# Routing all tokens in the first round, and gathering sorted tiles by a table of one-hot products

## The chip, the core and the metric

The kernel runs on one core of a Trainium2 chip. The metric is the device time of one execution in microseconds (us), as the median of several runs. TensorE is called PE here, VectorE DVE, ScalarE ACT, GpSimd POOL and SyncE SP, as in the profile. POOL issues the indirect DMAs and SP all the others.

## The reference, cut to what matters

The input `x` is 2 x 2048 tokens of 256 numbers. Two layers follow one another; each normalizes `x`, computes an attention branch `s` and a feed-forward branch `g`, and adds `s * silu(g)`. Only the first layer is touched:

```python
xn = _layernorm(x)
s = _L0_attn_ref(xn, ...)     # 16 heads, window of 128, plus 64 pooled latent keys, gated
g = _silu(_L0_ffn_ref(xn, ...))
x = x + s * g
```

`_L0_ffn_ref` is a mixture of experts with one expert for each token:

```python
expert_idx = argmax(softmax(x @ Wr.T))          # 8 experts
for e in range(8):
    inter += (expert_idx == e) * gelu(x @ W1[e] + b1[e])    # 256 -> 1024
y = inter @ Wo + bo + x                         # 1024 -> 256
out = (y - mean(y)) * rsqrt(var(y) + 1e-12) * gamma + beta
```

The second layer (a bucketed attention block, and a two-deep transformer of its own as the feed-forward branch) takes the rest of the time.

## The kernel before

**Tiling.** The 4096 tokens are 32 tiles of 128 (`NT`), taken in 8 groups of 4 (`NG`, `GT`). The first layer runs in eight rounds, one for each group `g`: the attention of the group's four tiles, and beside it whatever else is due. For the experts the tokens are sorted by expert, each expert's part padded to whole tiles of 128, so there are 39 sorted tiles at most (`FT = NT + E - 1`), and all 39 are always computed.

**Order of the work.** The instructions of PE, DVE, ACT and POOL stand in the order in which the program emits them; SP's DMAs are placed by the framework. `in_turn` (L90) takes lanes, each a list of steps with weights and a stretch from `a` to `b` of the round, gives each step a position in its lane's stretch by the weights, and emits all steps in order of position. So two numbers place each piece of work, and the engines run it in that order, each stalling where something is not there yet. A step emits all its instructions at once.

**The steps of the first layer.**
- `prep(g)` (L429): LayerNorm of a group on DVE with the reciprocal root on POOL, transposes on PE into `stream`, the eight router logits of each token, and the one-hot choice `oh`.
- `head(g)` (L649): projections of queries, keys and latent keys. `attention(g)` (L896): scores, softmax, weighted sums, gate, output; tile n's result is stored at L891 in the lane of tile n+1.
- `route()` (L473): from `oh` of all tokens, each token's place in the sorted order (`ati`) and each sorted tile's expert (`exi`). `ranks` uses two products on PE, the rest is DVE.
- `send(t)` (L546): one indirect DMA, from POOL, writes the 128 normalized rows of tile t to their places in `xsort` in DRAM. There are 32. `xsort` is filled with zeros at the start, so that the padding is defined.
- `open_experts` and `expert_load(i)` (L555, L563): `Wo` once; for a sorted tile the expert number is read into a register, then `w` (1 MB) and the tile's rows `xs` (from `xsort`) are loaded by SP. `expert(i)` (L571) does the two products with gelu between, and the normalization, and stores to `ysort`. Its `begin` asks for tile i+1. The results are fetched from `ysort` by `ati` in the next layer's `gate_head` (L341).

**The schedule of before.** Preps 0 and 1 and head 0 come before the first scores. Preps 2 to 4 lie in round 0, preps 5 to 7 and `route` in round 1, the sends from 0.7 of round 1 to 0.56 of round 2; the experts begin at 0.64 of round 2. `shares` says how much of a round holds experts:

```python
shares = [0, 0, 0.36, 1, 1, 1, 1, 0.7]
weight = sum(w for w, _ in flow) / sum(shares)
```

The pool `xp` holds the normalized rows of all groups (`xn`, 32 KB in each partition) until `open_experts` closes it; the weights of the experts then take its room.

Of the kernel before, what the change touches and what calls it, by code (L numbers as in the profile page):

```python
# [7 lines left out]
F32 = mybir.dt.float32  # L8
# [4 lines left out]
P = 128  # L13
# [17 lines left out]
def kernel(ctx: ExitStack, tc: tile.TileContext, io: dict, col: dict):  # L31
# [347 lines left out]
    with ExitStack() as l0_ctx, tc.manual_schedule(engines=ordered):  # L379
# [8 lines left out]
        xsort = dram.tile([FT * P, D], F32, name="xsort")  # L388
        x_ctx = ExitStack()
        xp = pool("xp", 1, "right", x_ctx)  # L390
        xn = sb(xp, [P, NT, D], "xn")
        for g in range(NG):
            nc.sync.dma_start(xn[:, g * GT : (g + 1) * GT, :], xin[:, g * GT : (g + 1) * GT, :])
            if g == 0:
                wr = sb(l0, [P, 2, E], "wr")
                nc.sync.dma_start(wr, io["WrT"].rearrange("(k p) e -> p k e", p=P))
                wqkv = sb(wa, [P, 2, 3 * D], "wqkv")
                nc.sync.dma_start(wqkv, io["L0_attn_qkv_w"].rearrange("(k p) n -> p k n", p=P))
                rqw = sb(wa, [P, 2, 64], "rqw")
                nc.sync.dma_start(rqw, io["L0_attn_rq_w"].rearrange("(k p) n -> p k n", p=P))  # L400
                rkvw = sb(wa, [P, 2, 128], "rkvw")
                nc.sync.dma_start(rkvw, io["L0_attn_rkv_w"].rearrange("(k p) n -> p k n", p=P))
                halves = load_halves(wa, "halves_a")
# [9 lines left out]
        mask_lat = cst_a[:, 384:512]  # L413
        desc = cst_a[:, 512:520]
        before = cst_a[:, 520:648]
        starts = cst_a[:, 648 : 648 + NT]
        places = cst_a[:, 648 + NT : 648 + NT + FT]
# [11 lines left out]
        def prep(g):  # L429

            d = {}
            xg = xn[:, g * GT : (g + 1) * GT, :]
            xT = xT_of(g)
            o = oh[:, g * GT : (g + 1) * GT, :]

            def moments(t):
                if not t:
                    d["mv"] = sb(xp, [P, GT, 2], "ln_mv", 3)
                    d["rs"] = sb(xp, [P, GT], "ln_rs", 3)
                ln_moments(xp, d["mv"], t, [xg[:, t, :]])  # L440

            def turn(c):
                tp = bank("tp")
                for t in range(GT):
                    nc.tensor.transpose(tp[:, t * P : (t + 1) * P], xg[:, t, c * P : (c + 1) * P], ident)
                copy(c, xT[:, c, :], tp)

            def logits():
# [20 lines left out]
            lane += [(1, lambda t=t: normalize(xg[:, t, :], xg[:, t, :], d["mv"], d["rs"], t)) for t in range(GT)]  # L469
            lane += [(1, lambda c=c: turn(c)) for c in range(2)] + [(1, lambda: None), (1, logits)]  # L470
            return lane

        def route():  # L473

# [50 lines left out]
            def places_of():  # L525

                row = d["row"]
                nc.vector.tensor_tensor(row, d["upto"], d["total"], ALU.subtract)
                nc.vector.tensor_tensor(row, row, d["rank"], ALU.add)
                nc.vector.tensor_tensor(row, row, bc(d["first"], 1, [P, NT, E]), ALU.add)  # L530
                nc.vector.tensor_tensor(row, row, oh, ALU.mult)
                at = sb(xp, [P, NT], "at")
                nc.vector.tensor_reduce(at, row, AX.X, ALU.add)
                nc.vector.tensor_copy(ati, at)

            def experts_of():
                past = sb(xp, [P, FT, E], "past")
# [25 lines left out]
        def expert_load(i):  # L563
            e = nc.sync.value_load(exi[0:1, i : i + 1], min_val=0, max_val=E - 1)
# [368 lines left out]
        sends = [(1, lambda t=t: send(t)) for t in range(NT)]  # L933
# [714 lines left out]
def _constants():  # L1648
# [14 lines left out]
    starts = np.broadcast_to(P * np.arange(NT), (P, NT))  # L1663
    places = np.broadcast_to(np.arange(FT), (P, FT))
    cst = np.concatenate([np.eye(P), mask_c, mask_d], 1).astype(np.float32)
    cst_a = np.concatenate([*mask_a, mask_lat, desc, i < j, starts, places], 1).astype(np.float32)

    f = np.float32
    half = np.arange(0, DH, 2, dtype=f)
# [120 lines left out]
```

## Time and profile before

| what | us |
|---|---|
| median of 5 runs | 3110.69 (3108.76 to 3114.71) |
| the profiled execution | 3114.44 |
| its span, first to last instruction | 3112.7 |

Busy over the span: PE 2755.2 us (89%), DVE 1885.2 (61%), ACT 1677.3 (54%), POOL 1064.7 (34%). The first layer takes the first 963 us or so. Busy time counts an engine that runs an instruction, not one that issues a DMA or waits. The granted clock (PEclk) is the share of full speed at which PE was let run; a stretch with a low clock has longer matmuls for the same work.

Lines of the profile name a source line and the tiles, written first: `tp<-cst,xs` at L580 is the transposes of a sorted tile's rows. A wait is told as who waited, for whom, the total, how often, and the longest.

### The profile page before, as it was taken

How to read it: one execution, taken by the hardware profiler on the slowest of the kernel's cores; microseconds unless marked ns; L12 is line 12 of the kernel's file. 1: busy time of each engine (PE TensorE's matmuls, PEld its weight loads, DVE VectorE, ACT ScalarE, POOL GpSimd, SP SyncE). 2: the span in 40 equal slices, each digit the busy share in tenths (PEclk: the TensorE clock that was granted, in tenths of full speed). 3: DMA queues.
4: the chain of work that ended last, by engine and by line, in shares of the span. 5: the costliest groups of instructions: out<-in, count | busy, mean ns of one | idle time of the engine just before them, and what ended most of it. 6: DMA issues, size and time to landing. Idle time of an engine off the chain costs nothing.

```text
span 3112.7 us, 72624 instructions
## 1 busy us (share of the span) xinstructions
PE 2755.2 (89%) x28250; PEld 1981.2 (64%) x28250; DVE 1885.2 (61%) x6708; ACT 1677.3 (54%) x4598; POOL 1064.7 (34%) x1227
## 2 busy tenths in 40 slices
PE   7776899999994789999999999999998689999997
PEld 4554778877882556655666666666665556666666
DVE  6775455545563777767676776666665375555542
ACT  4544667767771444444444445455553277667662
POOL 1224223323234554554443444444341112222212
PEclk8888999999996899999999999999999899999998
DMA  5001422222212000100000010000000100000000
GB/s 170 15 22 58 141 98 91 93 87 91 97 65 90 25 25 27 28 28 25 15 18 29 15 37 8 8 8 5 5 2 16 57 9 23 23 24 23 15 15 21
DMA packets 88418, 128.63 MB, mean 41 GB/s; under 512 B 8174, under 2 KB 78221, under 8 KB 83085
## 3 DMA queue, kind: packets, MB, share of 16 engines
q1 hardware_dynamic: 85004, 115.60, 11.6%
q0 software_dynamic: 3072, 8.39, 0.9%
q8 instruction: 225, 3.69, 0.5%
q14 instruction: 117, 0.95, 0.1%
HBM read 88.58 MB, written 27.00 MB: 37 GB/s over the span
## 4 chain that ended last, share of the span: by engine, by line
PE 32%; DVE 6%; issue 4%; POOL 4%; ACT 4%; DMA 0%; SPq 0%; POOLq 0%; DVEq 0%; ACTq 0%
PE s L1296 7%; PE s L1612 3%; PE s L1599 3%; PE s L1318 3%; PE s L1086 3%; ACT pr L1489 2%; PE s L1214 2%; POOL inv L1130 1%; PE s L1102 1%; PE acc L1041 1%; POOL scr L1119 1%; PE s L1011 1%; PE tp L151 1%; PE tp L1502 1%; PE s L1469 1%
## 5 line engine op out<-in xcount | busy, mean ns | idle before, releaser
L1031 ACT ACTIVATE pr<-pr,mn 128x192 f32<-128x192 f32 (+2 forms) x512 | 188.6, 439 | 277.5 <-DVE mn L107 273.5
L1130 POOL TENSOR_TENSOR inv<-inv,nhalf 128x16 f32<-128x16 f32 x64 | 188.4, 2944 | 414.6 <-DVE inv L1129 414.6
L107 DVE CUSTOM_DVE_ANT_0 pr<-s,cst 128x128 f32<-128x128 f32 (+2 forms) x1024 | 261.5, 316 | 102.3 <-PE s L1469 81.1
L1296 PE MATMUL s<-h2T,d_w 128*128 128x512 f32 (+2 forms) x792 | 317.4, 556 | 0.6 <-DVE h2T L1286 0.6
L69 ACT COPY pt<-tp 128x384 f32<-128x384 f32 (+3 forms) x320 | 156.3, 495 | 274.8 <-PE tp L151 253.4
L151 PE MATMUL tp<-cst,pr 128*128 128x128 f32 x1488 | 219.7, 285 | 61.7 <-ACT pr L1031 52.3
L136 ACT ACTIVATE pr<-pr,mn 128x192 f32<-128x192 f32 (+2 forms) x512 | 222.9, 436 | 67.5 <-DVE mn L107 67.1
L1489 ACT ACTIVATE pr<-pr,mn 128x128 f32<-128x128 f32 x512 | 198.1, 388 | 112.6 <-DVE mn L107 112.3
L1086 PE MATMUL s<-d_wqkv,hT 128*128 128x512 f32 x512 | 247.1, 627 | 0.0
L1119 POOL TENSOR_TENSOR scr<-scr,tab 128x512 f32<-128x512 f32 x128 | 176.8, 1381 | 202.0 <-DVE scr L71 201.9
L151 PEld LDWEIGHTS tp<-cst,pr 128*128 128x128 f32 x1488 | 180.1, 147 | 101.6 <-ACT pr L1031 58.1
L1296 PEld LDWEIGHTS s<-h2T,d_w 128*128 128x128 f32 x792 | 146.1, 198 | 141.9 <-issue 135.6
L71 DVE COPY pt<-tp 128x384 f32<-128x384 f32 (+3 forms) x320 | 181.3, 566 | 70.7 <-PE tp L151 52.1
L1309 DVE SCALAR_TENSOR_TENSOR u<-s,cols,ge 128x512 f32<-128x512 f32 (+2 forms) x108 | 74.0, 689 | 201.9 <-PE s L1296 130.9
L1318 PE MATMUL s<-d_w,u 128*128 128x256 f32 x768 | 177.9, 382 | 0.0
L1086 PEld LDWEIGHTS s<-d_wqkv,hT 128*128 128x128 f32 x512 | 99.3, 204 | 100.7 <-issue 100.0
L611 PE MATMUL s<-Wo,it 128*128 128x128 f32 x1248 | 158.5, 281 | 2.2 <-ACT it L603 1.3
L165 PE MATMUL acc<-pt,v 64*32 64x128 f32 x4992 | 123.2, 289 | 39.9 <-DVE pt L71 28.1
L1617 POOL TENSOR_TENSOR y<-y,stream 128x256 f32<-128x256 f32 x32 | 23.3, 729 | 391.9 <-DVE y L1616 391.9
L1318 PEld LDWEIGHTS s<-d_w,u 128*128 128x128 f32 x768 | 142.5, 190 | 22.5 <-issue 3.1
L611 PEld LDWEIGHTS s<-Wo,it 128*128 128x128 f32 x1248 | 149.3, 195 | 10.6 <-issue 6.8
L594 PE MATMUL s<-xsT,w 128*128 128x128 f32 x1248 | 149.2, 278 | 0.0
(271 smaller groups left out, 6403.6 us busy)
## 6 DMA issues: line engine op xcount, KB each, us to landing
w<-in_W1b_dram SPq DMA_DIRECT2D x39, 1028.0 KB
xsort<-zero SPq DMA_DIRECT2D x1, 4992.0 KB
xs<-xsort SPq DMA_DIRECT2D x39, 128.0 KB
ysort<-ys SPq DMA_DIRECT2D x39, 128.0 KB
xn<-in_L_attn_x_dram SPq DMA_DIRECT2D x8, 512.0 KB
rows_s<-s SPq DMA_DIRECT2D x32, 128.0 KB
stream<-in_L_attn_x_dram SPq DMA_DIRECT2D x8, 512.0 KB
sg<-rows_s SPq DMA_DIRECT2D x8, 512.0 KB
```

The source lines that it names most:

```text
L71: nc.vector.tensor_copy(out, in_)
L107: nc.vector.tensor_tensor_reduce(pr, sc, mask, 1.0, CAP, ALU.add, ALU.min, mn)
L136: nc.scalar.activation(w, w, AF.Exp, bias=mn[:, v : v + 1], scale=-1.0, accum_out=zs[:, v, blk, s : s + 1])
L151: nc.tensor.transpose(tp[:, k * P : (k + 1) * P], pr[:, k, :, :].rearrange("p v j -> p (v j)"), ident)
L611: nc.tensor.matmul(mm, lhsT=d["it"][:, ic, :], rhs=late["Wo"][:, ic, h], start=(ic == 0), stop=(ic == FF // P - 1))
L1031: nc.scalar.activation(p, p, AF.Exp, bias=mn[:, w : w + 1], scale=-1.0)
L1086: nc.tensor.matmul(mm, lhsT=heads[r][:, k, t * P : (t + 1) * P], rhs=wqkv_d[l][:, k, j * INNER : (j + 1) * INNER], start=(k == 0), stop=(k ...
L1119: nc.gpsimd.tensor_tensor(d["r2"][:, :, :, 32 * hf : 32 * hf + 32], d["qk"][:, :, :, 32 - 32 * hf : 64 - 32 * hf], bc(d["tab"][:, 2:4, hf, ...
L1130: nc.gpsimd.tensor_tensor(inv.rearrange("p a h -> p (a h)"), inv.rearrange("p a h -> p (a h)"), nhalf, ALU.pow)
L1296: nc.tensor.matmul(mm, lhsT=w1[l][:, k, c, :], rhs=d["h2T"][:, k, 0:w], start=(k == 0), stop=(k == 1))
L1318: nc.tensor.matmul(mm[:, 0:D], lhsT=d["u"][:, c, i * P : (i + 1) * P], rhs=w2[l][:, c, :], start=(c == 0), stop=(c == HC - 1),)
L1489: nc.scalar.activation(w, w, AF.Exp, bias=mn[:, v : v + 1], scale=-1.0, accum_out=zs[:, v, blk, st : st + 1])
```

## The change

- Four preps come before the first scores, the other four in the first half of round 0, `route` at 0.48 to 0.6 of round 0, `open_experts` and the first `expert_load` at 0.6 to 0.62, and the experts begin at 0.65 of round 0. They are spread over all later rounds.
- `xn` becomes four rotating buffers. Each group's normalized rows are stored to `rows_n` in DRAM, and the load of group g+4 follows the prep of group g.
- `xsort`, its zeros and the 32 sends are gone. In their place `route` makes `src`, the table of the token in each place of each sorted tile. `tiles_of` splits a token's place into tile `f` (one-hot, `past`) and row `p`; `tokens_of` sums, over the 32 token tiles, the product of the one-hot rows (128 x 128) with the one-hot tiles times the token's number (128 x 78, tile start and row kept apart). `expert_load` gathers `xs` from `rows_n` by `src`, with an indirect DMA from POOL.

```diff
-        for g in range(NG):
-            nc.sync.dma_start(xn[:, g * GT : (g + 1) * GT, :], xin[:, g * GT : (g + 1) * GT, :])
+        xn = {}
+        def load_x(g):
+            if g < NG:
+                xn[g] = sb(xp, [P, GT, D], "xn", 4)
+                nc.sync.dma_start(xn[g], xin[:, g * GT : (g + 1) * GT, :])
+        for g in range(4):
+            load_x(g)
...
-        zero = sb(wa, [P, D], "zero")
-        nc.vector.memset(zero, 0.0)
-        nc.sync.dma_start(xsort.rearrange("(n p) d -> p n d", p=P), bc(zero, 1, [P, FT, D]))
...
+            store = rows_n[g * GW : (g + 1) * GW, :].rearrange("(t p) d -> p t d", p=P)
+            lane.append((0, lambda: nc.sync.dma_start(store, xn[g])))
             lane += [(1, lambda c=c: turn(c)) for c in range(2)] + [(1, lambda: None), (1, logits)]
-            return lane
+            return lane + [(0, lambda: load_x(g + 4))]
...
+            def tiles_of():
+                past = sb(xp, [P, NT, FT + 1], "past_f")
+                nc.vector.tensor_tensor(past, bc(d["at"], 2, ...), bc(edges, 1, ...), ALU.is_ge)
+                f = sb(xp, [P, NT], "f")
+                nc.vector.tensor_reduce(f, past[:, :, 1 : FT + 1], AX.X, ALU.add)
+                p = d["p"] = sb(xp, [P, NT], "p")
+                nc.vector.tensor_scalar(p, f, -float(P), None, ALU.mult)
+                nc.vector.tensor_tensor(p, p, d["at"], ALU.add)
+                nc.vector.tensor_tensor(past[:, :, 0:FT], past[:, :, 0:FT], past[:, :, 1 : FT + 1], ALU.subtract)
+                d["past"] = past
+
+            def tokens_of():
+                mm = bank("s")[:, 0 : 2 * FT]
+                for g in range(NG):
+                    one = sb(xp, [P, GT, P], "one", 2)
+                    nc.vector.tensor_tensor(one, bc(d["p"][...], 2, ...), bc(along, 1, ...), ALU.is_equal)
+                    past = d["past"][:, g * GT : (g + 1) * GT, 0:FT]
+                    num = sb(xp, [P, GT, 2, FT], "num", 1)
+                    nc.vector.tensor_tensor(num[:, :, 0, :], past, bc(starts[...], 2, [P, GT, FT]), ALU.mult)
+                    nc.vector.tensor_scalar(num[:, :, 1, :], past, down, None, ALU.mult)
+                    for t in range(GT):
+                        n = g * GT + t
+                        nc.tensor.matmul(mm, lhsT=one[:, t, :], rhs=num[:, t, :, :]..., start=(n == 0), stop=(n == NT - 1))
+                both = sb(xp, [P, 2, FT], "both")
+                nc.vector.tensor_copy(both, mm.rearrange("p (a f) -> p a f", a=2))
+                nc.vector.tensor_tensor(both[:, 0, :], both[:, 0, :], both[:, 1, :], ALU.add)
+                nc.vector.tensor_copy(src, both[:, 0, :])
...
-            return [(1, ranks), (1, running), (1, ends), (1, places_of), (1, experts_of)]
-
-        def send(t):
-            nc.gpsimd.indirect_dma_start(
-                xsort, bass.IndirectOffsetOnAxis(ap=ati[:, t : t + 1], axis=0), xn[:, t, :], None
-            )
+            return [(1, f) for f in (ranks, running, ends, places_of, tiles_of, experts_of, tokens_of)]
...
-            nc.sync.dma_start(d["xs"], xsort[i * P : (i + 1) * P, :])
+            nc.gpsimd.indirect_dma_start(
+                d["xs"], None, rows_n, bass.IndirectOffsetOnAxis(ap=src[:, i : i + 1], axis=0)
+            )
...
-        in_turn((0, 1, prep(0)), (0.5, 1.5, prep(1)), (0.9, 1.8, head(0)))
+        in_turn(*((0.5 * g, 0.5 * g + 1, prep(g)) for g in range(4)), (0.9, 1.8, head(0)))
...
-        shares = [0, 0, 0.36, 1, 1, 1, 1, 0.7]
+        shares = [0.35, 1, 1, 1, 1, 1, 1, 0.7]
...
             if g == 0:
-                lanes += [(0.3 * k, 0.3 * k + 0.35, prep(2 + k)) for k in range(3)]
-            if g == 1:
-                lanes += [(0.16 * k, 0.16 * k + 0.25, prep(5 + k)) for k in range(3)]
-                lanes += [(0.6, 0.68, route()), (0.7, 1, sends[0:11])]
-            if g == 2:
-                lanes.append((0, 0.56, sends[11:]))
-                lanes.append((0.57, 0.62, [(1, open_experts)] + [(1, lambda: expert_load(0))]))
+                lanes += [(0.09 * k, 0.09 * k + 0.2, prep(4 + k)) for k in range(4)]
+                lanes += [(0.48, 0.6, route()), (0.6, 0.62, [(1, open_experts), (1, lambda: expert_load(0))])]
...
-                lanes.append((1 - shares[g] if g == 2 else 0, shares[g] if g == NG - 1 else 1, share))
+                lanes.append((0 if g else 1 - shares[g], shares[g] if g == NG - 1 else 1, share))
```

The constants grow by the edges of the sorted tiles (`edges`) and two counters (`along`, `down`).

More of the change, by code (lines that the diff above doesn't have):

```diff
@@ L387 @@
         exi = l0.tile([P, FT], I32, name="exi", tag="exi")
-        xsort = dram.tile([FT * P, D], F32, name="xsort")
+        rows_n = dram.tile([B * S, D], F32, name="rows_n")
+        src = l0.tile([P, FT], I32, name="src", tag="src")
         x_ctx = ExitStack()
         xp = pool("xp", 1, "right", x_ctx)
-        xn = sb(xp, [P, NT, D], "xn")
-        for g in range(NG):
-            nc.sync.dma_start(xn[:, g * GT : (g + 1) * GT, :], xin[:, g * GT : (g + 1) * GT, :])
+        xn = {}
[5 more added lines that the diff above has]
+            load_x(g)
             if g == 0:
@@ L415 @@
         before = cst_a[:, 520:648]
-        starts = cst_a[:, 648 : 648 + NT]
-        places = cst_a[:, 648 + NT : 648 + NT + FT]
+        edges = cst_a[:, 648 : 649 + FT]
+        starts = edges[:, 0:NT]
+        places = cst_a[:, 649 + FT : 649 + 2 * FT]
+        along, down = cst_a[:, 649 + 2 * FT : 777 + 2 * FT], cst_a[:, 777 + 2 * FT : 778 + 2 * FT]
         bout, gl, gr = rows[:, 0:256], rows[:, 256:272], rows[:, 272:288]
         bv, brout, brv = halves[:, 0:128], halves[:, 128:256], halves[:, 256:288]
-        zero = sb(wa, [P, D], "zero")
-        nc.vector.memset(zero, 0.0)
-        nc.sync.dma_start(xsort.rearrange("(n p) d -> p n d", p=P), bc(zero, 1, [P, FT, D]))
         bqe, bqo = masked_biases(wa, "a_bq")
@@ L431, in prep @@
             d = {}
-            xg = xn[:, g * GT : (g + 1) * GT, :]
             xT = xT_of(g)
@@ L439, in moments @@
                     d["rs"] = sb(xp, [P, GT], "ln_rs", 3)
-                ln_moments(xp, d["mv"], t, [xg[:, t, :]])
+                ln_moments(xp, d["mv"], t, [xn[g][:, t, :]])
             def turn(c):
@@ L444, in turn @@
                 for t in range(GT):
-                    nc.tensor.transpose(tp[:, t * P : (t + 1) * P], xg[:, t, c * P : (c + 1) * P], ident)
+                    nc.tensor.transpose(tp[:, t * P : (t + 1) * P], xn[g][:, t, c * P : (c + 1) * P], ident)
                 copy(c, xT[:, c, :], tp)
@@ L468, in prep @@
             lane += [(1, lambda: ln_rsqrt(d["rs"], d["mv"], 1e-5)), (2, lambda: None)]
-            lane += [(1, lambda t=t: normalize(xg[:, t, :], xg[:, t, :], d["mv"], d["rs"], t)) for t in range(GT)]
+            lane += [(1, lambda t=t: normalize(xn[g][:, t, :], xn[g][:, t, :], d["mv"], d["rs"], t)) for t in range(GT)]
+            store = rows_n[g * GW : (g + 1) * GW, :].rearrange("(t p) d -> p t d", p=P)
+            lane.append((0, lambda: nc.sync.dma_start(store, xn[g])))
             lane += [(1, lambda c=c: turn(c)) for c in range(2)] + [(1, lambda: None), (1, logits)]
-            return lane
+            return lane + [(0, lambda: load_x(g + 4))]
         def route():
@@ L531, in places_of @@
                 nc.vector.tensor_tensor(row, row, oh, ALU.mult)
-                at = sb(xp, [P, NT], "at")
+                at = d["at"] = sb(xp, [P, NT], "at")
                 nc.vector.tensor_reduce(at, row, AX.X, ALU.add)
                 nc.vector.tensor_copy(ati, at)
+            def tiles_of():
+                past = sb(xp, [P, NT, FT + 1], "past_f")
+                nc.vector.tensor_tensor(
+                    past, bc(d["at"], 2, [P, NT, FT + 1]), bc(edges, 1, [P, NT, FT + 1]), ALU.is_ge
+                )
[6 more added lines that the diff above has]
+                d["past"] = past
@@ new lines, in tokens_of @@
+            def tokens_of():
+                mm = bank("s")[:, 0 : 2 * FT]
+                for g in range(NG):
+                    one = sb(xp, [P, GT, P], "one", 2)
+                    nc.vector.tensor_tensor(
+                        one,
+                        bc(d["p"][:, g * GT : (g + 1) * GT], 2, [P, GT, P]),
+                        bc(along, 1, [P, GT, P]),
+                        ALU.is_equal,
+                    )
+                    past = d["past"][:, g * GT : (g + 1) * GT, 0:FT]
+                    num = sb(xp, [P, GT, 2, FT], "num", 1)
+                    nc.vector.tensor_tensor(
+                        num[:, :, 0, :], past, bc(starts[:, g * GT : (g + 1) * GT], 2, [P, GT, FT]), ALU.mult
+                    )
+                    nc.vector.tensor_scalar(num[:, :, 1, :], past, down, None, ALU.mult)
+                    for t in range(GT):
+                        n = g * GT + t
+                        nc.tensor.matmul(
+                            mm,
+                            lhsT=one[:, t, :],
+                            rhs=num[:, t, :, :].rearrange("p a f -> p (a f)"),
+                            start=(n == 0),
+                            stop=(n == NT - 1),
+                        )
+                both = sb(xp, [P, 2, FT], "both")
+                nc.vector.tensor_copy(both, mm.rearrange("p (a f) -> p a f", a=2))
+                nc.vector.tensor_tensor(both[:, 0, :], both[:, 0, :], both[:, 1, :], ALU.add)
+                nc.vector.tensor_copy(src, both[:, 0, :])
@@ L568, in expert_load @@
             d["xs"] = sb(pm[0], [P, D], "xs", 3)
-            nc.sync.dma_start(d["xs"], xsort[i * P : (i + 1) * P, :])
+            nc.gpsimd.indirect_dma_start(
+                d["xs"], None, rows_n, bass.IndirectOffsetOnAxis(ap=src[:, i : i + 1], axis=0)
+            )
         def expert(i):
@@ L930 @@
         flow = experts()
-        shares = [0, 0, 0.36, 1, 1, 1, 1, 0.7]
+        shares = [0.35, 1, 1, 1, 1, 1, 1, 0.7]
         weight = sum(w for w, _ in flow) / sum(shares)
-        sends = [(1, lambda t=t: send(t)) for t in range(NT)]
         for g in range(NG):
@@ L1662, in _constants @@
     desc = np.broadcast_to(E - np.arange(E), (P, E))
-    starts = np.broadcast_to(P * np.arange(NT), (P, NT))
+    edges = np.broadcast_to(P * np.arange(FT + 1), (P, FT + 1))
     places = np.broadcast_to(np.arange(FT), (P, FT))
     cst = np.concatenate([np.eye(P), mask_c, mask_d], 1).astype(np.float32)
-    cst_a = np.concatenate([*mask_a, mask_lat, desc, i < j, starts, places], 1).astype(np.float32)
+    cst_a = np.concatenate([*mask_a, mask_lat, desc, i < j, edges, places, np.broadcast_to(j, (P, P)), i], 1).astype(np.float32)
     f = np.float32
```

## The prediction

> **What bounds the kernel now.** I read the profile's page first, then busy times by stretch, then waits and single lines inside the first part. The page's slices are 77.8 us each:
>
> ```profile
> PE   7776899999994789999999999999998689999997
> ...
> PEclk8888999999996899999999999999999899999998
> ```
>
> The first three or four PE digits are 7 and 7 and 7 and 6, with a granted clock of 0.8; from slice five on PE is at 8 or 9 and the clock at 0.9 and above. The hole at slice 13 is the passage to the next layer. So the first layer has a thin part and a full part. The store of token tile n is issued when the lane of tile n+1 ends, so the eight stores that matter (129.4, 237.0, 361.4, 482.1, 601.4, 728.5, 855.0, 962.4 us) cut the layer into its rounds. Busy times in these stretches (start of round 0 at about 40 us):
>
> ```profile
> 40.00:130.00 90.00, 74.32 (x850) 53.55 (x850) 65.45 (x298) 55.89 (x227) 15.13 (x22) 0.83 0.03 10
> 130.00:238.00 108.00, 78.56 (x916) 56.59 (x916) 77.84 (x342) 53.19 (x209) 27.00 (x37) 0.84 0.07 23
> 238.00:362.00 124.00, 86.18 (x1030) 66.33 (x1031) 58.84 (x264) 63.18 (x233) 43.98 (x57) 0.85 0.29 99
> 362.00:483.00 121.00, 115.27 (x1355) 99.25 (x1355) 67.38 (x299) 83.98 (x283) 36.75 (x61) 0.99 0.28 94
> ...
> 729.00:856.00 127.00, 117.79 (x1376) 101.19 (x1375) 68.23 (x301) 89.46 (x286) 38.66 (x63) 0.99 0.28 94
> 856.00:963.00 107.00, 84.37 (x1051) 70.89 (x1049) 61.63 (x253) 63.12 (x202) 39.92 (x61) 0.89 0.21 67
> ```
>
> Columns: stretch and length, then busy time of PE, PE weight load, DVE, ACT, POOL, then clock and DMA. Rounds 3 to 6 hold experts in full and are PE-bound: 115 of 121 and 118 of 127 us. Rounds 0 to 2 leave PE idle for 16, 29 and 38 us, and what PE does runs at 0.83 to 0.85. Two waits of round 2 stand out:
>
> ```profile
> PE tp L580 <- DMA xs<-xsort: 17.4, 1, 17.4
> ```
> ```profile
>   DMA xsort<-xn,ati: 46.0, 27
> ```
>
> PE stood 17.4 us before the first sorted tile's rows came; and POOL, over its 32 sends, stood 46 us, as each waits for the landing of the one before.
>
> **What moves.** 39 sorted tiles go from 5.06 shares (7.7 tiles in a full round) to 7.05 shares: 1.9 tiles in round 0, 5.5 in each of rounds 1 to 6, 3.9 in round 7. Nothing else of the PE work leaves, so the gain can only be PE idle time, and each stretch is priced on its own.
>
> **The price of a sorted tile.** Its three groups of matmuls, over rounds 3 to 6:
>
> ```profile
> 362.00:856.00 494.00, 122.26 (x1020) 117.73 (x1019) 0.99 0.28 93
> ```
> ```profile
> 362.00:856.00 494.00, 127.44 (x1002) 120.55 (x1003) 0.99 0.28 93
> ```
> ```profile
> 362.00:856.00 494.00, 11.95 (x62) 7.83 (x62) 0.99 0.28 93
> ```
>
> These are L594, L611 and L580: 261.7 us for 1020/32, 1002/32 and 62/2, about 31.5 tiles, or 8.3 us a tile and 7.9 tiles a round.
>
> **Rounds 1 to 6.** A full round takes 494/4 = 123.5 us. With 2.4 tiles fewer, PE-bound all the way, it takes 123.5 - 2.4 x 8.3 = 104 us. Attention without experts has its own length: round 0's 90 us with three preps, or some 78 us without (a prep at 4 us, worked out below). The straight line from 78 us at no tile to 123.5 at 7.9 gives 110 us at 5.5; from 90 it gives 113. The truth lies between the line and the PE bound; I take 109, nearer the line, because the PE clock may slip when PE idles more (0.85 against 0.99). Today rounds 1 to 6 take 108 + 124 + 494 = 726 us; then 6 x 109 = 654 (624 to 678). That is 72 us gained. The sends (32 x 0.96 us of POOL and the 46 us of waits) and the first wait of 17.4 us go with it, already in those numbers.
>
> One rule of the Trainium skill bears on that clock: TensorE: Matmul & The Clock Gate, in "Why this matters for your kernels", says that the clock stays full as long as PE has no gap over about 3 us. By it rounds 1 to 6 would stay full and come to 104 to 106 us each, 18 to 30 us less in all. The rows here show means of 0.83 to 0.85 in the thin rounds without saying which gaps caused it.
>
> **Round 7** holds 3.9 tiles where it had 4.6 by the matmul counts: 0.7 x 8.3 = 6 us of PE; I take 7 with the thinner spread, 107 to 100 us (97 to 103). The tail that waits for the last sorted rows stays.
>
> **Prologue.** Preps 2 and 3 come before the first scores. A prep's DVE rows: 4 x (0.41 moments + 0.18 + 0.43 normalize) + 0.67 copy + 5 x 0.2 routing = 5.7 us, so 11.4. Against it DVE's wait of 2.9 us for the constants at 20 us should go: four x loads of 0.5 MB stand before them in place of eight, and the 5 MB of zeros are no longer written (DMA is 0.98 busy in the first 40 us). I take +8 (3 to 11.4). The eight new stores of normalized rows (0.5 MB each) and the late x loads lie in a stage with DMA 0.03 to 0.07 busy: nothing, or, were SP behind on its waits, a few us of prep, inside the next item's bounds.
>
> **Round 0** now holds four preps instead of three, all before its middle; the whole routing; and 1.9 sorted tiles from 0.65 on.
> - Fourth prep: 5.7 us of DVE, which is 65 of 90 us busy: +4 (0 to 5.7).
> - Routing as it is: DVE ran it for 9.4 us between 198 and 211 us, and the two tiles around it took 54 us where the two of round 0 took 46: +9 (8 to 11).
> - New in the routing, `tiles_of`: a compare of 1280 elements, a sum and a difference of 1248. No row has that size; by L538 (312 elements, 0.476 us) and L530 (256, 0.426) DVE takes about 1 ns an element and 0.15 us, so 1.4 + 1.4 + 1.4 + 0.4 = 4.6 us.
> - New, `tokens_of`: 8 groups in lockstep. `num` has one buffer, so DVE may not write the next before PE has read the last. Per group two products of 156 elements (0.6 us), a semaphore, then 4 products that PE runs as 8 load and matmul pairs of at least 0.12 us (L453: 16 pairs in 1.85 us, or 3.9 us when cold), then the way back: 2.0 us (1.9 to 2.5); `one` (512 elements, 0.67 us) hides behind PE. 16 us (15 to 20), and 0.8 us of final copies. All is emitted as one step, so the softmax rows of the attention behind it on DVE and every matmul behind it on PE wait, and through them ACT's copies and exponentials.
> - So +21 for both (10 if DVE's 25 idle us of the round take half; 25).
> - First sorted tile: Wo, w1 and the gather are asked for at 0.6 to 0.62 and wanted at 0.65. Before, first matmul minus w1 issue was 324.7 - 310.5 = 14 us, and the lane between is worth some 4. A register load on SP per tile stands in the way too, hidden today between 211 and 235 us:
>
> ```profile
> L564 SPq TENSOR_LOAD <-exi x39: 177/265/502, 211.3 to 234.7; - x39
> ```
>
>   Those 23 us begin with `exi`, some 18 us before the table is done, and the weight loads may queue behind them on SP. +10 (0 to 17.4).
> - 1.9 tiles x 8.3 = 16 us of PE, a part in idle time: +13 (8 to 16).
>
> Sum: 90 + 4 + 9 + 21 + 10 + 13 = 147 (130 to 165, since the ends do not all fall together).
>
> DVE's speed beside POOL matters to the new routing: L529 took 0.829 us while a POOL add ran from 207.08 to 207.92, its like L530 0.426 without one. POOL is busy 15 of 90 us in round 0, so some 2 us of the 13 DVE us could double; it is inside the 25. The Trainium skill, SBUF — State Buffer, "SBUF: two separate sides", has this as an exclusive lock between a DVE operation with two SBUF inputs and a GpSimd one; by it the gathers too would wait on DVE. That speaks against the change, by no more than these 2 us as I estimate it from the page.
>
> **Gathers.** The 39 loads of `xs` leave SP for POOL. Issue: 0.96 us as L547, 37 us over the layer against 31 for the sends, but with no wait for one another, one sorted tile (some 20 us) ahead of use, landing 2.4 to 2.7 us (L547, L341). POOL is 37 of 121 us busy in full rounds. Behind them wait `ys`'s add and the gates; covered: 0. If the cover failed, 39 x 1 us.
>
> **The sum**, in the profiled execution (3114.4 us, span 3112.7; the median of the runs is 3110.7, 0.12% lower): 40 + 8 + 147 + 654 + 100 = 949 us for the layer against 963, that is -14 us; the later layers are untouched. On the median: 3097 us.
>
> **The rivals.**
> - PE-bound rounds: 105 us each, round 0 at 135, round 7 at 98: 40 + 8 + 135 + 630 + 98 = 911, -52 us, 3059. For: the rounds at 95% PE. Against: idle of 16 us in round 0, where PE had little to wait for but attention's own chain.
> - Slower by the routing block: all of it sits in one chain, DVE to PE and back, in front of both attention and the first sorted tile. The balance turns at a round 0 of 161 us. At 175 (tokens 25 with cold clock, SP's register loads and weights 20 or more, no filling) it is +14 us, 3125. For: 17.4 us of wait at the same spot before; against: DVE and PE had slack there.
> - The change doesn't do what it says: thinner rounds don't get shorter, since attention's latency sets them. At 114 us (the line from 90) the sum is 40 + 8 + 147 + 684 + 101 = 980, +17 us, 3128. Against: tile 7 alone, without head or experts, took 16 us.
>
> **How the numbers follow.** Forecast 0.50, PE-bound 0.20, routing block 0.17, no shortening 0.13. A kernel like this one can be told from no change at about 0.2%, 6 us. Of the forecast's 0.50 some 0.10 fall within 6 us and 0.40 are faster; of the two slow cases 0.03 lie within. Faster 0.60, same 0.13, slower 0.27. The forecast's own range is 3080 to 3112; the range that holds 8 in 10 reaches to the PE-bound case and the slow ones: 3055 to 3130.
>
> **What would show it.** Right: round 0 of 147 us with PE idle in one block of 20 us or more around the 32 new products; rounds 1 to 6 near 109 us with PE 90% busy and a clock near 0.97; no POOL wait on gathers; store of the last tile near 949 us. Wrong: rounds 1 to 6 over 112 us or round 0 over 161; `xs` waits by PE after the first tile; SP's register loads ahead of w1 with PE idle for 20 us.

## The result: no change in the time, a thin start for full rounds

The changed kernel takes 3112.76 us (median of 25 runs, 3107.72 to 3119.18) beside 3111.37 us of the kernel before (46 runs, 3105.89 to 3115.88). The ratio is 1.0005, with a 95% interval of 0.9999 to 1.001. The forecast was 3097. The profiled execution took 3114.14 us, with a span of 3112.3 against 3112.7.

The page of the changed kernel, PE busy in tenths and the granted clock in slices of 77.8 us:

```profile
PE   6688999999984789999999999999998689999997
...
PEclk7689999999997899999999999999999799999999
```

Slices three and four, 7 and 6 before, are at 8, and the row of 9 begins one slice earlier. In return the first two fell from 7 and 7 to 6 and 6, and their clock from 8 and 8 to 7 and 6. The hole at the passage to the next layer stands at the same slice, 13: what came in and what went out cancel.

The stores of the token tiles show the same by round. Ends of rounds in the changed kernel: 222.8, 330.4, 439.9, 545.2, 654.6, 764.1, 870.3 and 965.9 us.

| stretch | before | forecast | after |
|---|---|---|---|
| up to the end of round 0 | 129.4 | 195 | 222.8 |
| rounds 1 to 6, together | 726 | 654 | 647.5 |
| round 7 | 107 | 100 | 95.6 |
| end of the layer | 962.4 | 949 | 965.9 |

Busy times by stretch, rounds 1, 3 and 7 of the changed kernel (columns as before: length, PE, PE weight load, DVE, ACT, POOL, clock, DMA):

```profile
223.00:330.00 107.00, 97.76 (x1201) 81.05 (x1201) 63.84 (x286) 75.45 (x256) 38.37 (x58) 1.00 0.26 87
...
440.00:545.00 105.00, 98.76 (x1220) 82.74 (x1218) 62.42 (x283) 76.74 (x265) 37.53 (x56) 1.00 0.25 78
...
870.00:966.00 96.00, 68.57 (x929) 55.18 (x927) 57.15 (x241) 53.78 (x183) 35.20 (x52) 0.91 0.16 50
```

PE is busy for 98 of 107 and 99 of 105 us at a clock of 1.00. The rounds are level and PE-bound, as the forecast had them. The loss is all ahead of them. The same view of the piece from the first value projection to the store of tile 0, and from there to the end of round 0; after:

```profile
47.50:129.10 81.60, 64.16 (x503) 47.02 (x504) 50.68 (x241) 34.01 (x144) 10.53 (x17) 0.63 0.09 31
129.10:222.80 93.70, 64.55 (x647) 54.24 (x647) 51.64 (x197) 35.80 (x131) 14.92 (x19) 0.76 0.23 77
```

and the same two pieces of the kernel before:

```profile
34.00:83.20 49.20, 38.96 (x434) 26.77 (x432) 36.12 (x190) 32.71 (x143) 7.16 (x12) 0.83 0.11 43
83.20:129.40 46.20, 38.27 (x481) 29.34 (x479) 33.61 (x151) 26.86 (x106) 8.39 (x12) 0.85 0.06 19
```

Three losses are to be read there. The first value projection (L228) begins at 47.6 us in place of 34.1: +13.5 us of prologue. The piece up to tile 0's store grew by 32 us. The rest of round 0 grew by 47.5 us, for the routing, the table and the sorted tiles that are new in it, although two of the three preps that round 0 held before no longer stand there; PE is idle for 29 of these 93.7 us, before for 8 of 46.2.

The second loss was not in the forecast. Four preps now lie in that piece. The groups of PE there, longest first (busy us, mean ns | idle before, releaser); after:

```profile
L457 PE MATMUL s<-wr,stream 128*128 128x8 f32 x65 | 13.2, 335 | 2.0 <-ACT stream L69 2.0
L449 PE MATMUL tp<-cst,xn 128*128 128x128 f32 x32 | 8.7, 375 | 9.3 <-DVE xn L88 8.4 <-PE tp L151 0.9
...
L204 PE MATMUL s<-stream,wqkv 128*128 128x512 f32 x8 | 7.0, 1029 | 0.0
```

and before:

```profile
...
L204 PE MATMUL s<-stream,wqkv 128*128 128x512 f32 x8 | 5.0, 758 | 0.0
...
L453 PE MATMUL s<-wr,stream 128*128 128x8 f32 x16 | 2.0, 257 | 0.0
L445 PE MATMUL tp<-cst,xn 128*128 128x128 f32 x8 | 1.6, 287 | 0.1
```

A prep is 8 transposes (L449) and 8 products for the router's logits (L457), and each product is two matmuls in fp32; before the change the same lines are L445 and L453. In the changed kernel they take 21.9 us of PE in this piece, before 3.6 us, so 18 us more. The rest of PE's busy time is some 7 us more (64.2 - 21.9 = 42.3 against 39.0 - 3.6 = 35.4): rows run slower (L204 at 1029 ns, before 758), and 2 us are the routing's first two products (L495), which are new here. PE's idle time rose by 7 us, from 10.2 to 17.4. That makes the 32 us. The waits of the same piece, after (total, times, longest):

```profile
POOL ln_rs L84 <- DVE ln_mv L80: 44.6, 3, 21.9
DVE mx L465 <- PE s L457: 13.9, 5, 4.0
...
PEld tp L449 <- DVE xn L88: 10.5, 9, 2.7
```

DVE stood 13.9 us for the logits, with the softmax rows of the attention queued behind that wait. PE's weight loads stood 10.5 us for normalized rows that DVE had not come to. POOL was busy for 10.5 of these 81.6 us; its 44.6 us are mostly lack of work.

### The profile page after: what moved, and what is told of

The parts are those of the page before. It is cut to its first block, busy times and chain, and to the rows that moved or that the text cites. A ratio compares the mean times of both kernels' runs of the same rounds, so it can differ in the third digit from the quotient of the medians.

```text
span 3112.3 us, 72694 instructions
## 1 busy us (share of the span) xinstructions
PE 2766.5 (89%) x28314; PEld 1993.4 (64%) x28314; DVE 1899.5 (61%) x6739; ACT 1677.5 (54%) x4600; POOL 1074.9 (35%) x1234
## 4 chain that ended last, share of the span: by engine, by line
PE 32%; DVE 7%; issue 4%; POOL 4%; ACT 4%; DMA 0%; SPq 0%; POOLq 0%; DVEq 0%; ACTq 0%
PE s L1338 7%; PE s L1654 3%; PE s L1641 3%; PE s L1360 3%; PE s L1128 3%; ACT pr L1531 2%; PE s L1256 2%; POOL inv L1172 1%; PE s L1144 1%; PE acc L1083 1%; POOL scr L1161 1%; PE s L1053 1%; PE tp L151 1%; PE tp L1544 1%; PE s L1511 1%
## 5 line engine op out<-in xcount | busy, mean ns | idle before, releaser
L151 PE MATMUL tp<-cst,pr 128*128 128x128 f32 x1488 | 216.5, 282 | 57.7 <-ACT pr L1073 51.3
L659 PE MATMUL s<-Wo,it 128*128 128x128 f32 x1248 | 156.5, 279 | 3.0 <-DVE mnl L107 3.0
L107 DVE CUSTOM_DVE_ANT_0 pr<-s,cst_a 128x192 f32<-128x192 f32 (+2 forms) x512 | 143.9, 346 | 14.1 <-PE s L114 11.4
```

Of the source, the lines that this page charges most:

```text
L107: nc.vector.tensor_tensor_reduce(pr, sc, mask, 1.0, CAP, ALU.add, ALU.min, mn)
L151: nc.tensor.transpose(tp[:, k * P : (k + 1) * P], pr[:, k, :, :].rearrange("p v j -> p (v j)"), ident)
L659: nc.tensor.matmul(mm, lhsT=d["it"][:, ic, :], rhs=late["Wo"][:, ic, h], start=(ic == 0), stop=(ic == FF // P - 1))
```

## The experiments

The theory was "crowding": four preps in two tiles cost PE and DVE far more than the 4 us that I gave a prep. Its rivals were the table itself, the cold clock, and waits in program order on DVE. The median of the kernel before lay between 3107.8 and 3111.4 us beside these runs, so the ratios decide. The edits are shown in part, against the changed kernel, and in the last two pairs of runs as the step from the first of the pair to the second. Each trace is of one execution.

**The table without the new schedule.**

```diff
-        in_turn(*((0.5 * g, 0.5 * g + 1, prep(g)) for g in range(4)), (0.9, 1.8, head(0)))
+        in_turn((0, 1, prep(0)), (0.5, 1.5, prep(1)), (0.9, 1.8, head(0)))
-        shares = [0.35, 1, 1, 1, 1, 1, 1, 0.7]
+        shares = [0, 0, 0.36, 1, 1, 1, 1, 0.7]
+                lanes += [(0.3 * k, 0.3 * k + 0.35, prep(2 + k)) for k in range(3)]
...
+                lanes.append((0.6, 0.68, route()))
```

> The table and the gathers in the schedule of before: two preps ahead of the scores, routing at 0.6 to 0.68 of round 1, weights at 0.57 to 0.62 of round 2, experts from 0.64 of round 2. This is the table in place of the sends with nothing else moved. Table costs 27 us of DVE and PE in round 1 (22 products, 5 tile numbers). Theory 'the sends were nearly free, POOL had room': rounds 1 and 2 take 231 + 27 - 10 (first sorted tile's wait) = 248, total 3125 to 3130. Theory 'the sends cost as much as the table' (46 us of POOL waits in front of the gates, and the 17.4 us wait of the first sorted tile): total within 5 us of before, 3106 to 3116.

Measured: 3107.73 us, ratio 0.9994 (0.9984 to 1.0004). Rounds end at 127.7, 263.3, 358.2 and 477.3 us, where before they ended at 129.4, 237.0, 361.4 and 482.1. Round 1 took 28 us longer (it holds the table) and round 2 29.5 us less (the sends and the first sorted tile's wait are gone). The table and the gathers by themselves cost what the sends cost.

**The new schedule without the table.** The sends of the kernel before, preps and routing where the change put them, experts from 0.56 of round 1. The lines of the sends themselves are those of the kernel before.

```diff
-        shares = [0.35, 1, 1, 1, 1, 1, 1, 0.7]
+        shares = [0, 0.44, 1, 1, 1, 1, 1, 0.7]
+        sends = [(1, lambda t=t: send(t)) for t in range(NT)]
...
-                lanes += [(0.48, 0.6, route()), (0.6, 0.62, [(1, open_experts), (1, lambda: expert_load(0))])]
+                lanes += [(0.48, 0.58, route()), (0.6, 1, sends[0:15])]
```

> The kernel before with the changed schedule only: four preps ahead of the scores, four in the first half of round 0, the routing at 0.48 to 0.58 of round 0, the 32 indirect sends from 0.6 of round 0 to 0.48 of round 1, the experts from 0.56 of round 1 (6.14 shares). Theory 'crowding': round 0 still takes far more than 90 us, ending at 185 or more without any table, layer near 980, total 3120 to 3130. Theory 'the table's block is the cost': round 0 ends near 160, total 3100.

Measured: 3116.02 us, ratio 1.0017 (1.0008 to 1.0027). Tile 0 was stored at 128.8 us (129.1 in the changed kernel) and round 0 ended at 183.6 us, with no table, no gather and no sorted tile in it, but with 15 of the sends:

```profile
47.50:128.80 81.30, 63.57 (x526) 46.46 (x527) 52.22 (x244) 34.53 (x145) 10.53 (x17) 0.69 0.00 1
128.80:183.60 54.80, 36.37 (x434) 25.81 (x432) 34.24 (x156) 25.67 (x104) 19.77 (x23) 0.78 0.13 45
```

The first value projection begins at 53.6 us in this run, so the first line holds 6 us of the prologue. The prologue is that much longer than in the changed kernel; all of `x` is still loaded at the start and the zeros are still written, with DMA 0.95 busy from 30 to 40 us where it is 0.33 in the changed kernel. From the projection on, the first piece takes 75 us with PE busy for 57.7, beside 81.6 and 64.2 in the changed kernel and 49.2 and 39.0 before. The run with three buffers below has the changed kernel's instructions up to there, and took 75 us as well. So tile 0 is as late without the table as with it.

My sum for round 0 without table and tiles was 40 + 8 + 90 + 4 + 9 = 151, so preps and routing together were 33 us too cheap. From the store of tile 0 to the end of round 0 the changed kernel takes 93.7 - 54.8 = 39 us more: the table, the first sorted tile and the 1.9 tiles, less what the 15 sends cost. I had 21 + 10 + 13 = 44. The execution in this trace was the slowest of its ten (3120.48 us), so these differences are good to a few us only.

**Preps as before, routing in round 1.** The table and the gathers stay; three preps in each of the rounds 0 and 1, experts from 0.77 of round 1.

```diff
-        shares = [0.35, 1, 1, 1, 1, 1, 1, 0.7]
+        shares = [0, 0.23, 1, 1, 1, 1, 1, 0.7]
...
+                lanes += [(0.3 * k, 0.3 * k + 0.35, prep(2 + k)) for k in range(3)]
+            if g == 1:
+                lanes += [(0.16 * k, 0.16 * k + 0.25, prep(5 + k)) for k in range(3)]
+                lanes += [(0.6, 0.72, route()), (0.72, 0.74, [(1, open_experts), (1, lambda: expert_load(0))])]
```

> Changed kernel with the preps where they were before (two ahead of the scores, three in round 0, three in round 1) and the routing with its table at 0.6 to 0.72 of round 1, the experts right behind it from 0.77 of round 1 (5.93 shares, 6.6 tiles a round). Theory 'crowding or cold clock early' : round 0 ends at 130 us as before, round 1 takes 107 + 22 (table) + 5 + 8 (first sorted tile) + 8 = 150, rounds 2 to 6 115 each, layer near 955, total 3102. Rival 'the routing block with its table costs the same wherever it stands, about 45 us, and the early preps cost little': round 1 takes 165 or more, total 3115 or more.

Measured: 3092.05 us, ratio 0.9938 (0.9921 to 0.9955). Tile 0 was stored at 82.3 us and rounds 0 and 1 ended at 127.3 and 274.5:

```profile
34.00:82.30 48.30, 39.25 (x402) 25.92 (x399) 35.13 (x188) 32.16 (x141) 6.74 (x10) 0.75 0.07 23
```

The first piece is back at 50 us (the value projection begins at 32.5, 1.5 us ahead of the line) with PE busy for 41, at a clock of 0.76. The table stands later, takes the same 20 us (216.8 to 236.7), and 19 us of the time are gained against the kernel before. So the table was not what took the gain; the place of the preps and the routing was. They moved together here, and the total does not part them. Ahead of tile 0's store, where of the routing only the first two products ever stood, it is the preps.

**The preps spread.** Four preps ahead as in the change, the other four 0.23 apart over round 0, routing at 0.02 to 0.14 of round 1.

```diff
-                lanes += [(0.09 * k, 0.09 * k + 0.2, prep(4 + k)) for k in range(4)]
-                lanes += [(0.48, 0.6, route()), (0.6, 0.62, [(1, open_experts), (1, lambda: expert_load(0))])]
+                lanes += [(0.23 * k, 0.23 * k + 0.3, prep(4 + k)) for k in range(4)]
+            if g == 1:
+                lanes += [(0.02, 0.14, route()), (0.14, 0.16, [(1, open_experts), (1, lambda: expert_load(0))])]
```

> Changed kernel with the four late preps spread over all of round 0 (starts 0.23 of a round apart) in place of its first half, the routing at 0.02 to 0.14 of round 1, and the experts from 0.19 of round 1. Prologue with four preps and table unchanged. Theory 'crowding' (each prep costs some 12 us where four stand in two tiles, and 4 to 6 where there is one in a tile): the result of tile 0 is stored at 100 to 110 us in place of 129, round 0 ends at 145 to 155, layer near 950, total about 3095. Theory 'the clock, once low, makes a prep cost 12 us anywhere in round 0': round 0 ends at 165 or more, total 3110 or more.

Measured: 3100.59 us, ratio 0.9964 (0.9949 to 0.9978); tile 0 stored at 102.4 us, rounds 0 and 1 ended at 156.5 and 310.7. DVE's wait for the logits fell from 13.9 to 1.0 us. With all eight preps done and neither routing nor table begun, round 0 ended 27 us later than before, where five were done: 9 us for each of the three. Two of them stand ahead of the value projection, which began 12.7 us later (46.8); the fourth in round 0 cost the other 14 us (12 us in the run with the same preps and a cheaper table, below), although it was spread, and why is open. For the crowded ones the runs give this: from the projection to tile 0's store, with three preps more than before and the routing's first two products, 32 us more in the changed kernel and 26 in the run with the sends, so 9 to 11 us each.

**A warm PE.** Dummy products of 512 columns (21 of them, which are 42 matmul records with a median of 592 ns) between the preps' transposes and behind the first scores; nobody reads their results.

```diff
+        def warm(k):
+            mm = bank("s")
+            for _ in range(k):
+                nc.tensor.matmul(mm, lhsT=ident, rhs=wqkv[:, 0, 0:512], start=True, stop=True)
...
             def turn(c):
+                if g >= 2:
+                    warm(2 if c == 0 else 1)
...
         score(1)
+        warm(3)
```

> Changed kernel with matmuls of 512 columns put in where PE has nothing to do early on (three pairs after the first scores, one to two pairs before the transposes of each prep from group 2 on); their results are not read. In the changed kernel the result of tile 0 is stored at 129.1 us (83.2 before), the clock granted between 40 and 90 us is 0.50 to 0.66, and the table's eight groups take 2.62 us each. Theory 'cold clock' (the early tiles are long because PE runs at half clock): the clock rises to 0.9 or more, the store comes at 105 to 112 us, round 0 ends near 200 instead of 223, total 20 us less than the changed kernel, about 3092. Theory 'crowding' (four preps in two tiles, each step waiting in order on DVE, POOL and PE; the low clock is only the consequence): the clock rises, but the store stays at 125 to 135 us and the total at 3112 to 3120.

Measured: 3106.5 us, ratio 0.9984 (0.9974 to 0.9995); tile 0 stored at 120.4. Busy times in two windows of 20 us, the changed kernel:

```profile
40.00:60.00 20.00, 13.92 (x94) 11.02 (x96) 10.96 (x69) 8.39 (x45) 0.00 (x0) 0.50 0.23 79
60.00:80.00 20.00, 15.41 (x130) 11.29 (x131) 14.56 (x72) 10.43 (x45) 4.20 (x8) 0.50 0.09 29
```

and the warm one:

```profile
40.00:60.00 20.00, 15.60 (x152) 9.82 (x150) 13.88 (x86) 10.78 (x54) 1.97 (x5) 1.00 0.24 78
60.00:80.00 20.00, 16.20 (x112) 9.92 (x112) 13.88 (x61) 9.20 (x39) 2.24 (x3) 0.83 0.08 27
```

The clock column went from 0.50 and 0.50 to 1.00 and 0.83, and tile 0 came 9 us earlier although PE had work added. The ratio is 0.21% under the changed kernel's, so the cold clock is part of the loss, not most of it. How many us of tile 0 it is cannot be read here: the run with three buffers below stored tile 0 at 121.7 without any dummies.

**DVE off the logits.** VectorE's five router steps in a step of their own, behind other tiles' work.

```diff
+            def choose():
+                lg = d["lg"]
                 mx = sb(xp, [P, GT], "mx", 2)
...
-            lane += [(1, lambda c=c: turn(c)) for c in range(2)] + [(1, lambda: None), (1, logits)]
+            lane += [(1, lambda c=c: turn(c)) for c in range(2)] + [(1, lambda: None), (1, logits), (4, lambda: None), (1, choose)]
```

> The changed kernel with VectorE's five router steps (the top-2 and the one-hot rows) put into a step of their own, four weights after the matmuls that make the logits, so that VectorE does other tiles' work in between. Theory 'waits in order': VectorE stood 13.9 us for the logits between 47.5 and 125 us, and what stood behind it stood too; tile 0 is then stored at 115 to 120 us in place of 129 and the median is 8 to 12 us less, 3101 to 3105. Rival 'TensorE at half its clock is the limit of tiles 0 and 1': less than 3 us, 3110 to 3113, with tile 0 stored at 126 or later and a granted clock of about 0.5 between 40 and 80 us.

Measured: 3102.32 us, ratio 0.9977 (0.9968 to 0.9987); tile 0 stored at 115.9, as the theory of waits in order had it. The wait of DVE for the logits is no longer in the list. The clock of 60 to 80 us rose as well, to 0.63, so the two causes are not apart yet.

**Both.** The dummies and the moved router steps together.

```diff
+                if g >= 2:
+                    warm(2 if c == 0 else 1)
...
+            lane += [(1, lambda c=c: turn(c)) for c in range(2)] + [(1, lambda: None), (1, logits), (4, lambda: None), (1, choose)]
...
+        warm(3)
```

> The changed kernel with both edits: the dummy 512-column products of the warm kernel (their results are read by nobody) and VectorE's router steps moved away from the logits. If the clock and the waits in order are two shares of tiles 0 and 1, they add: tile 0 stored at about 107 us (129.1 less 8.7 and 13.2), the median at 3096. Rival, one share seen twice (VectorE waits because the products run at half clock): tile 0 stored at 114 to 118, the median at 3101 to 3104.

Measured: 3098.64 us, ratio 0.997 (0.9958 to 0.9981); tile 0 stored at 111.9, between the two forecasts. From the first score to that store: 79.6 us in the changed kernel, 73.1 warm, 68.2 split, 63.6 with both; so 6.5 and 11.4 apart and 16.0 together, nearly the sum. But the run with three buffers, with neither edit, has 73.1 as well, so single executions do not show that the two add. The ratios say less: 0.21%, 0.28% and 0.35% below the changed kernel's 1.0005, well under the sum, each with some 0.1% of uncertainty to either side. How clock and waits share the loss stays open. At a granted clock of 1.00 from 40 to 80 us and without that wait the piece still takes 15 us more than before (48.1).

**The table's lockstep.** Three buffers for `num` and `one`.

```diff
-                    one = sb(xp, [P, GT, P], "one", 2)
+                    one = sb(xp, [P, GT, P], "one", 3)
...
-                    num = sb(xp, [P, GT, 2, FT], "num", 1)
+                    num = sb(xp, [P, GT, 2, FT], "num", 3)
```

> Changed kernel with three buffers for the products' right sides and one-hot rows in place of one and two, so that DVE may run ahead of PE in making the table. Theory 'lockstep': the eight groups go from 2.62 us each to what PE needs, about 1.7 us at half clock, total 6 to 8 us less, 3105. Rival 'PE at half clock is the bound of these groups anyhow' : below 2 us less.

Measured: 3102.03 us, ratio 0.997 (0.9958 to 0.9983). The table's matmuls take 13.4 us (143.7 to 157.2) in place of 20, and PE has no gap in them:

```profile
143.70:157.20 13.50, 13.50 (x64) 13.50 (x64) 7.67 (x21) 0.00 (x0) 0.00 (x0) 0.50 0.00 1
```

Not all of the 0.35% is the table's: tile 0, which comes ahead of it, was stored at 121.7, with the same instructions on the engines up to there as in the changed kernel. The clock came up earlier in that execution:

```profile
60.00:80.00 20.00, 14.96 (x143) 9.90 (x139) 15.02 (x71) 10.94 (x45) 3.48 (x7) 0.65 0.08 28
```

It was 0.65 where the changed kernel's was 0.50, and I know of no other difference in that part, so I put its 7 us down to the clock.

**Three buffers and bf16 with the routing in round 1.** First the buffers alone, then the one-hots and the right sides in bf16 as well.

```diff
-                    one = sb(xp, [P, GT, P], "one", 3)
+                    one = xp.tile([P, GT, P], BF16, name="one", tag="one", bufs=3)
...
-                    num = sb(xp, [P, GT, 2, FT], "num", 3)
+                    num = xp.tile([P, GT, 2, FT], BF16, name="num", tag="num", bufs=3)
```

> The run with the routing in round 1, and three buffers for the products' right sides and one-hot rows. Theory 'lockstep': 64 matmuls of the table in some 14 us in place of 20, total 6 us less than that run, 3086. Rival (attention fills the difference): within 2 us of it, 3092.

> The same with one-hot rows and right sides in bfloat16 (their values, 0 or 1, multiples of 128 up to 3968 and numbers up to 127, are exact in it), so that each of the 32 products is one pass on PE in place of two. If PE at half clock bounds the table without the lockstep: DVE's 1.3 us a group is the bound then, the table takes 11 us, total 10 us less than with the lockstep, 3082. If the DVE work bounds it: as the run with three buffers, 3086.

Measured: 3086.52 us, ratio 0.9917 (0.99 to 0.9934), and 3082.81 us, ratio 0.9911 (0.9895 to 0.9928). The table's matmuls took 13.5 us (220.1 to 233.6) and then 7.4 us (217.3 to 224.7). The group in its bf16 form is half as many matmuls:

```profile
L576 PE MATMUL s<-num,one 128*128 128x78 bf16 x32 | 3.4, 253 | 9.8 <-DVE num L573 9.8
```

In fp32 it was 64 of 431 ns in the changed kernel. Now DVE bounds the table:

```profile
217.30:224.70 7.40, 3.05 (x31) 2.47 (x32) 7.24 (x21) 0.00 (x0) 0.00 (x0) 0.50 0.01 2
```

It is busy for 7.24 of the 7.4 us, and PE for 3.05. The intervals of these two kernels overlap, as do those of the first and of the run without its buffers, so neither step is shown by the times; the rows of the table show both.

**Spread preps with the cheap table, then six preps in round 0.**

```diff
-        in_turn(*((0.5 * g, 0.5 * g + 1, prep(g)) for g in range(4)), (0.9, 1.8, head(0)))
+        in_turn((0, 1, prep(0)), (0.5, 1.5, prep(1)), (0.9, 1.8, head(0)))
...
-                lanes += [(0.23 * k, 0.23 * k + 0.3, prep(4 + k)) for k in range(4)]
+                lanes += [(0.145 * k, 0.145 * k + 0.25, prep(2 + k)) for k in range(6)]
```

> The kernel with the late preps spread over round 0 (routing at the start of round 1), and with it three buffers for the table's partial results and bf16 for the one-hots and the right sides of the table's matmuls. If the table's price is the same wherever it stands (20 us in fp32, 7.4 us in bf16), this is some 10 us less than the spread kernel, 3090 (layer 937). Rival: at the start of round 1 the routing's chain and the rows of the gather set the end and not the table's matmuls: less than 4 us, 3097 to 3101.

> The same with two preps ahead of round 0 in place of four: six preps 0.145 of a tile-round apart over round 0, routing at 0.02 to 0.14 of round 1, the experts from 0.19 of it, bf16 and three buffers. If a prep costs what it crowds, and spread ones cost 4 to 6 us each: tile 0 stored before 100 us, round 0 ends at some 145, median about 3080. Rival (a prep costs 12 us each beyond the third wherever it stands): round 0 ends at 165 or later and the median is 3095 or more.

Measured: 3084.72 us, ratio 0.9919 (0.9902 to 0.9935), and 3077.0 us, ratio 0.9892 (0.9876 to 0.9909). The first is 16 us under the spread kernel (0.45% by the ratios); its layer ends 15 us earlier (932.9 against 947.7), of which 2 us lie in round 0, which holds no table. The other 13 us are what bf16 and the buffers took from the table's matmuls: they ran from 184.3 to 204.2 us in the spread kernel and from 182.3 to 189.7 here, so the table's price is the same at the start of round 1. The second is the fastest version here, faster than both kernels. From the first to the second only preps change their place, two of them from ahead of the scores into round 0; that is 7.7 us by the medians, with intervals that overlap. Its tile 0 was stored at 95.4 us and its round 0 ended at 148.2:

```profile
40.00:148.00 108.00, 88.71 (x920) 65.23 (x921) 80.43 (x351) 56.34 (x225) 18.94 (x28) 0.78 0.14 48
148.00:289.00 141.00, 105.88 (x1227) 86.55 (x1226) 85.72 (x344) 78.37 (x264) 35.98 (x50) 0.85 0.25 85
289.00:398.00 109.00, 102.15 (x1245) 85.82 (x1243) 66.05 (x288) 79.90 (x267) 38.74 (x59) 1.00 0.25 86
```

Three preps more than in the kernel before took 148.2 - 129.4 = 18.8 us, 6.3 each. DVE (80 of 108 us) and PE (89) are both well used, and from 289 us on the rounds are full. The forecast for the theory was 145 and 3080.

## Why the prediction was wrong

**What held.** Rounds 1 to 6 came to 107.9 us each, with 109 forecast, and round 7 to 95.6 with 100; rounds 1 to 7 together became 90 us shorter than before, with 79 forecast. PE is 91 to 94% busy there. No PE wait for `xs` stands behind the first tile's, so the gathers are covered; POOL stood 3.5 us for `xs`, twice. Of SP's 39 register loads 24 ran from 149.7 to 163.9 us, and SP then waited 8.1 us for the table; the other 15 came behind the first weights, so they did not delay these. The "no shortening" rival is out. So is the routing block's 20 us and more for weights and register loads: the weights were asked for at 172 and 173.5 us, the gathers landed, and PE's single wait there was 5.9 us.

**The step that failed** is "Fourth prep: 5.7 us of DVE, which is 65 of 90 us busy: +4", and with it "a prep at 4 us" and the prologue's "+8 (3 to 11.4)". At these prices tile 0 would have been stored at 83.2 + 8 + 3 x 4 = 103 us, since three preps more than before stand in its piece, and the rest of round 0 would have taken 46.2 - 2 x 4 + 9 + 21 + 10 + 13 = 91 us. Measured were 129.1 and 93.7. So 26 of the 28 us by which round 0 ended late lie ahead of the store of tile 0, and what the forecast had for the routing, the table and the sorted tiles came out right in sum, partly by luck: in the run with the sends the routing and 15 sends took 8 us more than I gave the routing, and the table and the tiles 5 us less than their 44.

Two preps in the prologue cost 13.5 us, outside my bounds. The three more in the piece behind it cost 9 to 11 us each, crowded; three more in round 0 cost 6.3 each where six were spread over it. The price was built from DVE rows alone. A prep also holds 24 matmuls and a chain DVE, POOL, DVE, PE, ACT or DVE, PE, DVE in which each engine works in order. The profile of before showed that PE part: 3.6 us a prep at a clock of 0.83. In the changed kernel it is 5.5 us a prep (21.9 us for four, at 0.63). "DVE is 65 of 90 us busy" was an average over a round, while the four preps fell into its first two tiles. That moving the router steps on DVE and adding the dummies each bring some of it back is shown; how much each holds is not.

**The table.** `tokens_of` took 22.2 us (149.9 to 172.1) with 16 forecast. Its rows in the changed kernel:

```profile
L575 PE MATMUL s<-num,one 128*128 128x78 f32 x64 | 16.0, 431 | 8.5 <-DVE num L572 8.5
...
L569 DVE TENSOR_TENSOR num<-past_f,cst_a 128x156 f32<-128x156 f32 x8 | 2.6, 322 | 10.4 <-PE s L575 10.4
```

A group's eight matmuls keep PE for 2 us, and then DVE and PE stand for each other (10.4 and 8.5 us in all): 2.6 us a group in place of 2.0. I had taken a warm clock for most of it, and it was 0.50 throughout. `tiles_of` took 4.8 us with 4.6 forecast. As the whole of table and tiles came to some 39 us with 44 forecast, this term did not decide. The one block of 20 us of idle PE that was to show the forecast right is not there: PE stood 9.5 us while DVE worked the routing, 8.5 us among its matmuls and 5.9 us before the first sorted tile.

**Of the rivals**, the routing block had the right figure, a round 0 of 175 us (47.6 to 222.8), but the wrong mechanism: 26 of the 28 us of excess lie ahead of tile 0's store, where only its first two products stand, and tile 0 is as late (128.8 us) when the table is taken away.

**The rules of the Trainium skill.** The text drew on TensorE: Matmul & The Clock Gate for the thin rounds. In rounds 1 to 6, with PE idle for 6 to 9 us a round and never for more than 2.1 us at once, the clock was 0.97 to 1.00, in agreement. Ahead of them it was not so: in the changed kernel the clock fell from 1.00 to 0.50 at 39.1 us and stayed there to 83.5, with no gap of PE over 0.8 us in the 19 us before the fall and none over 2.5 us after it. The same page, in "What's actually happening", has the clock full after some 3.4 us of sustained work. In the run with three buffers 13.5 us of the table's matmuls without a gap stayed at 0.50, so a PE that the profile shows busy is not enough, and with the dummies of 512 columns the clock was 1.00. The measurement decides. SBUF — State Buffer, on the lock between a two-input DVE operation and POOL, agreed: L535 to L537 (256 elements) took 0.83 us each beside POOL's three operations on 256 elements (L918 to L920), where the 256-element row of before took 0.426 alone. That cost 1.2 us.

## What to carry to other kernels

When work moves into a stage, price it on every engine that it runs on, and against the slack of the very tiles that it falls into, not of the round. Where a moved block has a chain that crosses engines in order, where it is placed within the stage can cost more than the block itself: here a prep cost 9 to 11 us crowded, and 6 us where six were spread over the round. Then test the schedule and the mechanism apart: each alone was worth nothing here, while the table, in bf16 and with three buffers, with six preps spread over round 0 and the routing behind them, was worth 1.1%.

## What the runs showed of the hardware

Matmuls without a gap for 13.5 us, each of 128 x 78 in fp32, did not raise the granted clock from 0.50. From 40 to 80 us of the changed kernel PE was busy for 29 of the 40 us, also at 0.50. With dummy products of 512 columns (42 matmuls from 33.7 to 109.7 us) added, it was 1.00 from 40 to 60 us and 0.83 from 60 to 80. With the same instructions, an early stage of thin PE work took 79.6 us in one execution and 73.1 in another, the clock being 0.50 and 0.65 from 60 to 80 us. A 128 x 78 product took two matmuls of 431 ns in fp32 and one of 253 ns in bf16, both at a clock of 0.50.
